# Five of eight activation transposes moved from TensorE to 32x32 block transposes on VectorE

## The chip, the core and the metric

The kernel runs on one core of a Trainium2 chip. The metric is the time of one execution on the device in microseconds; lower is better. A core has TensorE (PE, with its weight loads shown apart as PEld), VectorE (DVE), ScalarE (ACT), GpSimd (POOL) and SyncE (SP), which run their own programs in order and wait for each other through semaphores. SP and POOL issue the DMAs here, ACT four at the start.

## What is computed

Four batches of 512 tokens with 512 columns go through one layer of two halves, all in fp32:

```python
x = x + layernorm(attn(layernorm(x)))      # gated scan over the tokens
x = x + layernorm(ffn(layernorm(x)))

# attn: h [b, t, 512]
i, f, g = h @ Wi.T, h @ Wf.T, h @ Wg.T
gate = sigmoid(f);  v = silu(i) * (1 - gate)
o_t = gate_t * o_(t-1) + v_t               # associative scan over t
o = rmsnorm(o) * gnorm_w * g * sigmoid(g)
attn = einsum("btd,hd->bth", o, Wo)

# ffn: h [b, t, 512], 2048 hidden
hidden = silu(h @ W1.T) * (h @ W3.T)
ffn = hadamard(hidden) @ W2.T              # Walsh-Hadamard over the 2048
```

The kernel folds the Hadamard transform into W2. The products with Wi, Wf, Wg, W1 and W3 sum over the 512 columns of the normalized activations, so those must lie on the partitions: the normalized tile, with its tokens on the partitions, has to be transposed. There are two normalized tensors for each batch, called "a" (before attention) and "f" (before the FFN): eight transposes in all.

## The kernel before

**Products.** Every large product is done in seven block products instead of eight (Strassen-Winograd on a 2x2 split). `combine_left` and `combine_right` make the sums of blocks on DVE; `seven` returns the seven steps. A step is eight matmuls of 128x256, and its PSUM bank is then copied out by ACT (`nc.scalar.copy`, L348) or added in by DVE (L346). [...]

**Units.** `attn_unit(b, u)` is one of three attention units of batch b, `ffn_unit(b, m)` one of eight FFN units. Both call `project`, which runs the seven steps; after steps 1, 3, 5 and 6 (or after each, where `dense` is set, as in batch 0's FFN) `slot()` takes one piece of other work from the queue `fill`: the attention output of the next batch, the FFN output of this one, or the preparation of W2. The main loop runs over the batches b, and in it over m. After the eight FFN units of batch b come the three attention units of batch b+2, so that PE has work while DVE and ACT finish a batch. The attention units of batches 0 and 1 come ahead of the loop.

**Order.** The programs of PE and SP are in the order of the code (`manual_schedule`). Those of DVE, ACT and POOL are set by a scheduler from priorities and its own costs. `tc.high_priority` raises pieces of work.

**Normalizing.** `normalize_tiles` takes mean and variance on DVE (L244, L245), a power on POOL (L221) and writes (x - m) / s with one ACT instruction for each 128 tokens (L248) into a tile with tag "wide", of which there are three: xn, the attention output y and the FFN output f share them.

**Transposing.** `transpose` (L301) does 16 PE transposes of 128x128 into four PSUM banks (L309), two copies by ACT (L314), two by DVE (L316), and four combinations by DVE, at high priority. `xt`, the result, has two buffers. In the loop it is called for (b+2, "a") and (b+1, "f") one after the other at the end of each batch's FFN units, and for ("f", 3) alone at the end of batch 2.

**Weights.** `weight` loads a pair of column blocks of a weight from DRAM the first time (L157), 512 bytes for each row, with partition p holding rows p, 128 + p, 256 + p and 384 + p. DVE combines it, POOL stores it with its sums (`kept`, L138), and later batches load that (`again`, L145). In batch 0's FFN units SP's loads of new weights wait for buffers, and so for POOL's stores.

The functions that the change touches, and what calls them:

Of the kernel before, what the change touches and what calls it, by code (L numbers as in the profile page):

```python
# [11 lines left out]
F32 = mybir.dt.float32  # L12
AF = mybir.ActivationFunctionType
ALU = mybir.AluOpType
P = 128
# [12 lines left out]
B11, B21, B22, B12, T1, T2, T4 = range(7)  # L28
# [14 lines left out]
def kernel(  # L43
# [14 lines left out]
    nc = tc.nc  # L58
    B, T, D = x.shape
    FF = w1.shape[1]  # L60
    NT = T // P
    ND = D // P
    NF = FF // P
    NU = NF // 2
    NS = 2
    H = T // 2
# [7 lines left out]
    work = ctx.enter_context(tc.tile_pool(name="work", bufs=1))  # L74
    small = ctx.enter_context(tc.tile_pool(name="small", bufs=2))
    psum = ctx.enter_context(tc.tile_pool(name="psum", bufs=8, space=bass.MemoryType.PSUM))
    scratch = ctx.enter_context(
        tc.tile_pool(name="scratch", bufs=1, space=bass.MemoryType.DRAM)
    )
# [5 lines left out]
    def bank(name):  # L85
        return psum.tile([P, 2, H], F32, tag="ps", name=name)
# [18 lines left out]
    def flush():  # L105
        while fill:
            slot()


    xs = {}  # L110
# [16 lines left out]
    def combine_right(t, eng):  # L127

        eng.tensor_sub(t[:, T1], t[:, B12], t[:, B11])
        eng.tensor_sub(t[:, T2], t[:, B22], t[:, T1])  # L130
        eng.tensor_sub(t[:, T3], t[:, B22], t[:, B12])
        eng.tensor_sub(t[:, T4], t[:, B21], t[:, T2])
# [7 lines left out]
    def stream_tile(key, b, pool=stream):  # L140
        return pool.tile([P, 7, H], F32, tag="w", name="_".join(map(str, (*key, b))))

    def again(key, b, pool=stream):
        t = stream_tile(key, b, pool)
        nc.sync.dma_start(out=t, in_=saved[key])  # L145
        return t

    def weight(src, name, m, b):

        key = name, m  # L150
        if key in saved:
            return again(key, b).rearrange("p s (c f) -> p s c f", c=2)
        t = stream_tile(key, b)
        half = src.shape[1] // 2
        for h in range(2):
            cols = slice(h * half + m * P, h * half + (m + 1) * P)
            nc.sync.dma_start(  # L157
                out=t[:, 2 * h : 2 * h + 2].rearrange("p k (c f) -> p (k c) f", c=2),
                in_=src[:, cols].rearrange("(c p) f -> p c f", p=P),
            )  # L160
        uncombined.append((key, t))
        return t.rearrange("p s (c f) -> p s c f", c=2)
# [17 lines left out]
    def load_ffn_w(b, m):  # L180
        ffn_w[b, m] = weight(w1, "w1", m, b), weight(w3, "w3", m, b)
# [42 lines left out]
    def scales(mv, eps, name):  # L224

        n = mv.shape[1]
        r = inverse_root(mv, eps, name)
        nb = small.tile([P, n], F32, tag="nb", name=f"nb_{name}", bufs=4)
        i = nc.vector.scalar_tensor_tensor(nb, mv[:, :, 0], -1.0, r, ALU.mult, ALU.mult)
        return r, nb, i  # L230

    xns = {}

    def normalize_tiles(b, name, i0, n):

        if (name, b) not in xns:
            xns[name, b] = work.tile(
                [P, NT, D], F32, tag="wide", name=f"xn_{name}_{b}", bufs=3
            )
        t = xns[name, b]  # L240
        st = small.tile([P, n, 6], F32, tag=f"st{n}", name=f"st_{name}_{b}_{i0}")
        mv = small.tile([P, n, 2], F32, tag=f"mv{n}", name=f"mv_{name}_{b}_{i0}")
        for k in range(n):
            nc.vector.bn_stats(st[:, k, :], xs[b][:, i0 + k, :])  # L244
            nc.vector.bn_aggr(mv[:, k, :], st[:, k, :])  # L245
        r, nb, read["nb"] = scales(mv, EPS, f"{name}_{b}_{i0}")
        for k in range(n):
            nc.scalar.activation(  # L248
                t[:, i0 + k, :], xs[b][:, i0 + k, :], AF.Identity,
                bias=nb[:, k : k + 1], scale=r[:, k : k + 1],  # L250
            )

    def normalize(b, name, n=2):
        for i in range(0, NT, n):
            normalize_tiles(b, name, i, n)
# [43 lines left out]
    xts = {}  # L299

    def transpose(b, name):  # L301

        xn = xns.pop((name, b))
        xt = work.tile([P, 7, 2, H], F32, tag="xt", name=f"xt_{name}_{b}", bufs=2)
        pt = [bank(f"pt_{name}_{b}_{c}") for c in range(ND)]
        for h in range(2):
            for i in range(2 * h, 2 * h + 2):
                for c in range(ND):
                    nc.tensor.transpose(pt[c][:, h, ts(i % 2, P)], xn[:, i, ts(c, P)], ident)  # L309
        with tc.high_priority(offset=URGENT):  # L310
            for c in range(ND):
                to = xt[:, B11 : B12 + 1 : B12 - B11] if c < 2 else xt[:, B21 : B22 + 1]
                if c % 2:
                    nc.scalar.copy(to[:, :, c % 2, :], pt[c])  # L314
                else:
                    nc.vector.tensor_copy(to[:, :, c % 2, :], pt[c])  # L316
            combine_right(xt, nc.vector)
        xts[name, b] = xt


# [64 lines left out]
    def attn_unit(b, u, dense=False):  # L385
        def gates(d):

            v, gate = d[:, 0], d[:, 1]
            nc.scalar.activation(gate, gate, AF.Tanh, scale=0.5)
            nc.scalar.activation(v, v, AF.Silu)  # L390
            nc.vector.scalar_tensor_tensor(v, gate, 1.0, v, ALU.subtract, ALU.mult)
            nc.scalar.activation(gate, gate, AF.Identity, bias=half_t, scale=0.5)
            if u == 0:
                os_[b] = work.tile([P, 2, 2, T], F32, tag="o", name=f"o_{b}")
            for h in range(2):
                nc.vector.tensor_tensor_scan(
                    os_[b][:, u, h, :], gate[:, h, :], v[:, h, :], 0.0, ALU.mult, ALU.add
                )

        def output_gate(d):  # L400
            o = os_[b]
            og = work.tile([P, 7, 2, H], F32, tag="og", name=f"og_{b}")
            nc.scalar.activation(d, d, AF.Silu)
            for m in range(2):
                into_left(og, o[:, m], d[:, m], m)
            combine_left(og, nc.vector)
            ogs[b] = og
            nc.scalar.activation(o, o, AF.Square)
            nc.vector.tensor_add(o[:, 0], o[:, 0], o[:, 1])
            nc.vector.tensor_add(o[:, 0, 0], o[:, 0, 0], o[:, 0, 1])  # L410

        project(
            attn_w.pop((b, u)), xts["a", b], f"a_{b}_{u}", gates if u < 2 else output_gate,
            dense,
        )
# [52 lines left out]
    def ffn_unit(b, m, dense=False):  # L468
        def hidden(d):
            nc.scalar.activation(d[:, 0], d[:, 0], AF.Silu)  # L470
            ht = work.tile([P, 7, H], F32, tag="ht", name=f"ht_{b}_{m}", bufs=4)
            into_left(ht, d[:, 0], d[:, 1])
            combine_left(ht, nc.vector)
            hts[b, m] = ht

        project(ffn_w.pop((b, m)), xts["f", b], f"f_{b}_{m}", hidden, dense)
# [181 lines left out]
    for b in range(B):  # L658
        last = b == B - 1
        for m in range(NU):  # L660
            if m + 1 < NU:
                load_ffn_w(b, m + 1)
            if b == 0 and m % NS == 0:
                for k in range(m, m + NS):
                    fill.extend(transform_low(k))
            if m == 0 and not last:
                fill.extend([None] * 4 * (b > 0) + attn_out(b + 1))
            if m and m % NS == 0:
                if last and m == NU - NS:
                    fill.extend([None] * 8)  # L670
                fill.extend([None] + ffn_out(b, m // NS - 1))
            if m % NS == 1:
                load_down_w(b, m // NS)
            if m == 3 and b == 0:
                load_x(2)
            if m == 4 and b + 2 < B:
                normalize(b + 2, "a")
            ffn_unit(b, m, b == 0)
            combine_weights()
        tail = ffn_out(b, NU // NS - 1)  # L680
        if b + 2 < B:
            load_attn_w(b + 2, 0)
            transpose(b + 2, "a")
            transpose(b + 1, "f")
            fill.extend([None] + tail)
            for u in range(3):
                if u < 2:
                    load_attn_w(b + 2, u + 1)
                else:
                    load_ffn_w(b + 1, 0)  # L690
                attn_unit(b + 2, u)
            if b + 3 < B:
                load_x(b + 3)
        elif not last:
            load_ffn_w(b + 1, 0)
            transpose(b + 1, "f")
            fill.extend([None] + tail)
        else:
            fill.extend(tail)
            flush()  # L700
# [34 lines left out]
```

## Time and profile before

| | us |
|---|---|
| Median of 3 runs | 850.07 (849.54 to 850.56) |
| The profiled execution | 850.16 |
| Its span, first to last instruction | 848.2 |
| PE busy in the span | 824.5 (97%) |
| DVE / ACT / POOL busy | 452.7 (53%) / 263.5 (31%) / 60.6 (7%) |
| DMA moved | 159.06 MB, 187 GB/s from and to DRAM |
| Granted PE clock | 0.996 |

The profile is of one execution. A group of instructions is shown by line, engine, operation and tiles, with its count, busy time and mean; "idle before" is the time that its engine stood idle just ahead of it, with the instruction that ended the wait. A matmul's duration contains its latency, and matmuls overlap, so the time that a series takes is read from the starts of its neighbours or from the chain of work that ended last.

### The profile page before, as it was taken

Reading aid. Unit: us, or ns where it says so; the run is one execution under the profiler, and the core shown is the slowest. Engines: PE = TensorE matmul, PEld = TensorE weight load, DVE = VectorE, ACT = ScalarE, POOL = GpSimd, SP = SyncE. Lnnn points to the kernel's source line nnn. Section 1 sums busy time; section 2 is a strip of 40 time slices with the busy share of each in tenths; the row PEclk is TensorE's granted clock in tenths of the full one; section 3 lists DMA queues with packets and bytes.
Section 4 is the critical chain, followed back from the end, with each engine's and each line's share of the span. In section 5 each row is a group of like instructions: output and inputs, shape, how many; then the busy total and the mean of one; then the engine's idle time right before and its main releaser. Section 6 shows DMA issues by size and latency. Waiting matters only on the chain.

```text
span 848.2 us, 9895 instructions
## 1 busy us (share of the span) xinstructions
PE 824.5 (97%) x3808; PEld 710.1 (84%) x3808; DVE 452.7 (53%) x904; ACT 263.5 (31%) x386; POOL 60.6 (7%) x102
## 2 busy tenths in 40 slices
PE   6999999999999999999999999999999999999995
PEld 3778878888878888888888888888888888888884
DVE  5557686765564646537333645737334533633445
ACT  4454462433221224326211222524221211222111
POOL 4110110111100001002000000101000000100000
PEclk9999999999999999999999999999999999999998
DMA  9985376677778224826324322844251633625101
GB/s 339 402 308 216 134 271 230 223 273 273 273 287 326 87 87 171 361 88 236 128 114 188 116 87 87 301 182 174 87 208 43 270 140 122 223 88 216 49 40 50
DMA packets 53744, 159.06 MB, mean 188 GB/s; under 512 B 4289, under 2 KB 29505, under 8 KB 53697
## 3 DMA queue, kind: packets, MB, share of 16 engines
q1 hardware_dynamic: 45968, 120.40, 38.9%
q0 software_dynamic: 7008, 36.71, 10.8%
q10 hardware_dynamic: 720, 1.31, 0.4%
q8 instruction: 30, 0.49, 0.2%
q14 instruction: 18, 0.14, 0.0%
HBM read 120.66 MB, written 37.75 MB: 187 GB/s over the span
## 4 chain that ended last, share of the span: by engine, by line
PE 69%; DVE 2%; DMA 1%; ACT 1%; issue 1%; SPq 0%; POOLq 0%; DVEq 0%
PE X_f L361 21%; PE X_po L494 11%; PE Z_f L361 11%; PE Z_po L494 6%; PE Y_f L361 5%; PE X_a L361 5%; PE Y_po L494 3%; PE Z_a L361 2%; PE X_y L447 2%; PE Y_a L361 1%; PE Z_y L447 1%; DMA w<-in_W_dram 1%; DMA s_w<-w 1%; DVE f L346 0%; PE Y_y L447 0%
## 5 line engine op out<-in xcount | busy, mean ns | idle before, releaser
L361 PE MATMUL X_f<-xt_f,w 128*128 128x256 f32 x1024 | 241.9, 380 | 1.7 <-DVE xt_f L316 1.2
L361 PEld LDWEIGHTS X_f<-xt_f,w 128*128 128x128 f32 x1024 | 194.0, 190 | 32.5 <-issue 3.8
L348 ACT COPY d_f<-X_f 128x512 f32<-128x512 f32 x96 | 56.0, 584 | 306.1 <-PE X_f L361 281.7
L494 PE MATMUL X_po<-w,ht 128*128 128x256 f32 x512 | 120.9, 379 | 0.2 <-DVE f L346 0.2
L361 PE MATMUL Z_f<-xt_f,w 128*128 128x256 f32 x512 | 120.9, 379 | 0.0
L361 PEld LDWEIGHTS Z_f<-xt_f,w 128*128 128x128 f32 x512 | 97.3, 190 | 14.9 <-issue 1.0
L494 PEld LDWEIGHTS X_po<-w,ht 128*128 128x128 f32 x512 | 97.2, 190 | 13.7 <-DVE f L346 0.6
L346 DVE TENSOR_TENSOR f<-X_po,f 128x512 f32<-128x512 f32 x51 | 35.2, 689 | 97.0 <-PE X_po L494 96.9
L376 DVE TENSOR_TENSOR ht<-d_f 128x1024 f32<-128x1024 f32 x32 | 39.0, 1220 | 74.6 <-ACT d_f L470 55.4
L494 PE MATMUL Z_po<-w,ht 128*128 128x256 f32 x256 | 60.6, 379 | 1.5 <-DVE f L346 1.5
L361 PE MATMUL Y_f<-xt_f,w 128*128 128x256 f32 x256 | 60.5, 379 | 0.0
L494 PEld LDWEIGHTS Z_po<-w,ht 128*128 128x128 f32 x256 | 48.6, 190 | 8.5 <-DVE f L346 1.9
L361 PEld LDWEIGHTS Y_f<-xt_f,w 128*128 128x128 f32 x256 | 48.6, 190 | 8.3 <-issue 1.2
L348 ACT COPY d_a<-X_a 128x512 f32<-128x512 f32 x36 | 21.0, 584 | 92.4 <-PE X_a L361 76.3
L221 POOL TENSOR_TENSOR rs_f<-rs_f,power 128x2 f32<-128x2 f32 x16 | 14.6, 915 | 476.8 <-DVE nm_f L282 443.0
L346 DVE TENSOR_TENSOR d_f<-Z_f,d_f 128x512 f32<-128x512 f32 x32 | 22.1, 690 | 27.2 <-PE Z_f L361 27.2
L346 DVE TENSOR_TENSOR d_f<-X_f,d_f 128x512 f32<-128x512 f32 x32 | 22.1, 690 | 27.0 <-PE X_f L361 27.0
L361 PE MATMUL X_a<-xt_a,wi 128*128 128x256 f32 x128 | 33.1, 381 | 1.7 <-DVE xt_a L316 1.7
L470 ACT ACTIVATE d_f<-d_f 128x1024 f32<-128x1024 f32 x32 | 33.8, 1055 | 0.9
L361 PE MATMUL X_a<-xt_a,wf 128*128 128x256 f32 x128 | 32.9, 379 | 0.0
L346 DVE TENSOR_TENSOR f<-Z_po,f 128x512 f32<-128x512 f32 x28 | 19.3, 689 | 24.6 <-PE Z_po L494 24.6
L361 PE MATMUL X_a<-xt_a,wg 128*128 128x256 f32 x128 | 30.4, 381 | 1.4 <-DVE d_a L346 0.8
(150 smaller groups left out, 997.0 us busy)
## 6 DMA issues: line engine op xcount, KB each, us to landing
w<-s_w SPq DMA_DIRECT2D x80, 896.0 KB, 6.2
s_w<-w POOLq DMA_DIRECT2D x24, 896.0 KB, 4.8
w<-in_W_dram SPq DMA_DIRECT2D x32, 256.0 KB, 5.8
wi<-s_wi SPq DMA_DIRECT2D x6, 896.0 KB, 9.7
wf<-s_wf SPq DMA_DIRECT2D x6, 896.0 KB, 6.7
wg<-s_wg SPq DMA_DIRECT2D x6, 896.0 KB, 5.9
wo<-s_wo SPq DMA_DIRECT2D x6, 896.0 KB, 8.2
w_h<-w2p POOLq DMA_DIRECT2D x8, 512.0 KB, 7.3
```

Source lines behind the costliest of these rows:

```text
L221: read["power"] = nc.gpsimd.tensor_tensor(r, r, power_t[:, 0:n], ALU.pow)
L346: read[what] = nc.vector.tensor_add(to, ps[which], to)
L348: nc.scalar.copy(to, ps[which])
L361: nc.tensor.matmul(ps[:, n, :], w[:, a, c, :], xt[:, bb, c, :], start=first and n == 0 and c == 0, stop=c == 1, skip_group_check=True,)
L376: nc.vector.tensor_mul(to.rearrange("p (t k) f -> p k t f", t=2), a.rearrange("p k (t f) -> p k t f", t=2), b2.rearrange("p k (t f) -> p k ...
L447: nc.tensor.matmul(ps[:, t, :], og[:, a, c, ts(t, P)], w[c][:, bb, :], start=first and t == 0 and c == 0, stop=c == 1, skip_group_check=True,)
L470: nc.scalar.activation(d[:, 0], d[:, 0], AF.Silu)
L494: nc.tensor.matmul(ps[:, t, :], hts[b, m][:, a, ts(t, P)], w[m][:, bb, :], start=first and t == 0 and m == ms[0], stop=m == ms[-1], skip_g ...
```

## The change

Three of the eight transposes stay on PE: "a" of batches 0 and 1 and "f" of batch 0 (`ON_TENSOR`), all ahead of the main loop. The other five go another way:

1. ACT writes the normalized columns in another order, and POOL stores the tile to DRAM (`xnd`), in two DMAs of 512 KB.
2. `load_fold` loads it back on SP in four DMAs of 256 KB, one for each group of 32 partitions, in pieces of 512 bytes. Partition 32 i + q then holds columns 128 i to 128 i + 127 (in the new order) of every token whose number is q modulo 32. The tile has the tag "wide".
3. `transpose_fold` transposes 32x32 blocks on DVE, four instructions of 512 columns, which gives xt; the four combinations follow. Neither has a raised priority.

For block transposes to give rows that match, the 512 columns are dealt to the partitions as p = column // 4, so the weights' rows are loaded so too, and the three tensors that stay on PE are written by ACT with the matching order. In the loop, the fold that is needed first after batch b ("a" of b+2, or "f" of 3) is loaded at m = 6 and transposed at m = 7; "f" of b+1 is loaded after the units, ahead of the second attention unit's weights, and transposed ahead of that unit.

```diff
@@ weight @@
-                in_=src[:, cols].rearrange("(c p) f -> p c f", p=P),
+                in_=src[:, cols].rearrange("(p c) f -> p c f", p=P),
@@ normalize_tiles @@
+    ON_TENSOR = ("a", 0), ("a", 1), ("f", 0)
...
         for k in range(n):
+            x_t, to = xs[b][:, i0 + k, :], t[:, i0 + k, :]
+            if (name, b) in ON_TENSOR:
+                x_t = x_t.rearrange("p (k c) -> p c k", c=ND)
+                to = to.rearrange("p (c k) -> p c k", c=ND)
+            else:
+                x_t = x_t.rearrange("p (i a c) -> p i c a", c=ND, a=32)
+                to = to.rearrange("p (i c a) -> p i c a", c=ND, a=32)
             nc.scalar.activation(
-                t[:, i0 + k, :], xs[b][:, i0 + k, :], AF.Identity,
-                bias=nb[:, k : k + 1], scale=r[:, k : k + 1],
+                to, x_t, AF.Identity, bias=nb[:, k : k + 1], scale=r[:, k : k + 1]
+            )
+        if (name, b) not in ON_TENSOR:
+            if (name, b) not in xnd:
+                xnd[name, b] = scratch.tile(
+                    [NT, P, D], F32, tag=f"xn_{name}_{b}", name=f"xnd_{name}_{b}"
+                )
+            nc.gpsimd.dma_start(
+                out=xnd[name, b][i0 : i0 + n].rearrange("t p d -> p t d"),
+                in_=t[:, i0 : i0 + n, :],
             )
@@ new @@
+    def load_fold(b, name):
+        folds[name, b] = t = work.tile(
+            [P, T // 32, P], F32, tag="wide", name=f"fold_{name}_{b}", bufs=3
+        )
+        rows = xnd[name, b].rearrange("t p d -> (t p) d")
+        for i in range(4):
+            nc.sync.dma_start(
+                out=t[ts(i, 32)],
+                in_=rows[:, ts(i, P)].rearrange("(g q) k -> q g k", q=32),
+            )
+
+    def transpose_fold(b, name):
+        fold = folds.pop((name, b)).rearrange("p (h g) k -> p h g k", h=2)
+        xt = work.tile([P, 7, 2, H], F32, tag="xt", name=f"xt_{name}_{b}", bufs=2)
+        for c in range(ND):
+            to = xt[:, B11 : B12 + 1 : B12 - B11] if c < 2 else xt[:, B21 : B22 + 1]
+            nc.vector.transpose(
+                to[:, :, c % 2, :].rearrange("p h (g q) -> p h g q", q=32),
+                fold[:, :, :, ts(c, 32)],
+            )
+        combine_right(xt, nc.vector)
+        xts[name, b] = xt
@@ main loop @@
+            if m == 6 and not last:
+                load_fold(*((b + 2, "a") if b + 2 < B else (b + 1, "f")))
+            if m == NU - 1 and not last:
+                transpose_fold(*((b + 2, "a") if b + 2 < B else (b + 1, "f")))
             ffn_unit(b, m, b == 0)
...
         if b + 2 < B:
             load_attn_w(b + 2, 0)
-            transpose(b + 2, "a")
-            transpose(b + 1, "f")
+            load_fold(b + 1, "f")
             fill.extend([None] + tail)
             for u in range(3):
...
+                if u == 1:
+                    transpose_fold(b + 1, "f")
                 attn_unit(b + 2, u)
...
         elif not last:
             load_ffn_w(b + 1, 0)
-            transpose(b + 1, "f")
             fill.extend([None] + tail)
```

More of the change, by code (lines that the diff above doesn't have):

```diff
@@ L230, in scales @@
         return r, nb, i
-    xns = {}
+    xns, xnd = {}, {}
+    ON_TENSOR = ("a", 0), ("a", 1), ("f", 0)
     def normalize_tiles(b, name, i0, n):
@@ L317, in transpose @@
             combine_right(xt, nc.vector)
+        xts[name, b] = xt
+    folds = {}
+    def load_fold(b, name):
[18 more added lines that the diff above has]
+        combine_right(xt, nc.vector)
         xts[name, b] = xt
```

## The prediction

> **What bounds the kernel now.** I read the page first: busy times, then the chain that ended last.
>
> ```profile
> span 848.2 us, 9895 instructions
> ...
> PE 824.5 (97%) x3808; PEld 710.1 (84%) x3808; DVE 452.7 (53%) x904; ACT 263.5 (31%) x386; POOL 60.6 (7%) x102
> ...
> PE 69%; DVE 2%; DMA 1%; ACT 1%; issue 1%; SPq 0%; POOLq 0%; DVEq 0%
> ```
>
> TensorE is busy for 97% of the span, and of the chain no other engine holds more than 2%. DVE, ACT and POOL have room. So a PE instruction taken out shortens the run by its own pitch, provided nothing else becomes late in its place. The groups view, shapes kept apart, has the rows that go and the row that changes (busy, mean ns | idle before):
>
> ```profile
> L248 ACT ACTIVATE xn_f<-x,nb_f,rs_f 128x512 f32<-128x512 f32 x16 | 12.5, 808 | 14.8 <-DVE nb_f L229 14.8
> ...
> L309 PE MATMUL pt_f<-ident,xn_f 128*128 128x128 f32 x64 | 7.9, 273 | 0.1
> ...
> L316 DVE COPY xt_f<-pt_f 128x512 f32<-128x512 f32 x8 | 5.3, 686 | 1.8 <-PE pt_f L309 1.8
> ...
> L314 ACT COPY xt_f<-pt_f 128x512 f32<-128x512 f32 x8 | 4.3, 587 | 3.2 <-PE pt_f L309 3.2
> ```
>
> The 273 ns is a latency; matmuls overlap. The price in time is the pitch, which the chain in order of time gives:
>
> ```profile
> 282.23 1.75 PE pt_a L309 x16
> 283.98 1.75 PE pt_f L309 x16
> 285.73 1.73 PE X_a L361 x8
> ```
>
> Sixteen transposes cost 1.75 us, and after the first batch's two sets the matmuls go on without a gap. Then the timeline, for what PE waits for around transposes and at the start (start, duration, idle before and its releaser):
>
> ```profile
> 11.38 2.93 ACT L248 ACTIVATE xn_a<-x,nb_a,rs_a 128x512 f32<-128x512 f32 x4
> ...
> 12.24 2.77 PE L309 MATMUL pt_a<-ident,xn_a 128*128 128x128 f32 x16 [1.39 <-ACT xn_a L248]
> ...
> 15.47 1.13 PE L361 MATMUL X_a<-xt_a,wi 128*128 128x256 f32 x4 [0.46 <-DVE xt_a L316]
> ...
> 107.87 1.99 PE L361 MATMUL X_a<-xt_a,wg 128*128 128x256 f32 x8 [0.62 <-ACT d_a L348]
> ...
> 233.64 1.99 PE L494 MATMUL Z_po<-w,ht 128*128 128x256 f32 x8 [1.51 <-DVE f L346]
> ...
> 475.30 1.40 PEld L309 LDWEIGHTS pt_f<-ident,xn_f 128*128 128x128 f32 x13 [0.37 <-ACT xt_a L314]
> ...
> 674.25 1.99 PE L361 MATMUL X_f<-xt_f,w 128*128 128x256 f32 x8 [0.75 <-DVE xt_f L316]
> ```
>
> The last two are PE idle caused by the transposes that go: 0.37 for banks that ACT has not yet emptied, 0.75 for xt's copies. The first three lines are a part of the kernel where PE runs behind ACT: the four L248 activations, 0.73 us apart, set when the first matmuls can start.
>
> [...] No DVE transpose is in this trace. [...] The new activations read fp32 at a step of four elements[...]; no row of this trace reads so. [...] The trace's nearest loads, w<-in_W_dram with the same 512-byte pieces and 256 KB, land in 5.8 us (median).
>
> **The change, part by part.**
>
> *Transposes taken off PE.* Five sets (a of batches 2 and 3, f of 1, 2 and 3), 5 x 16 transposes: 5 x 1.75 = -8.75. The program of the changed kernel has 80 PE rows fewer and the same matmuls in the same order. The waits of 0.37 and 0.75 go with them: -1.12. What is late next at these places is nothing that I can see: each fold's transposes are issued in unit 7 or in the attention unit before the first use, a unit of 11 products x 1.73 = 19 us ahead.
>
> *DVE.* Per set it loses two copies of 686 ns and gains four block transposes[...] What hides it is idle DVE: over 434 to 454 us, where the set of batch 3 goes, DVE is busy 7.5 of 20 us. The transposes carry normal priority and stand in DVE's program between evacuations, which come 3 to 5 us apart there. Cost 0; if that cover fails, up to 0.5 us a set. ACT loses ten copies of 587 ns, off the path.
>
> *Stores (POOL).* Two per set, 512 KB, ten at the 0.53 to 0.58 us that POOL takes for s_w; POOL is 7% busy. Behind the first store of an f stands the pow of its second half, and DVE waits for that. In batch 2 the store can go at 392.2 plus whatever ACT adds, the pow ran at 394.1: no wait. In batch 0 the two a-stores (about 213 to 216 us) go ahead of w2's block 5, whose landing at 222.5 SP waits for before it loads unit 6's weights; that is the chain behind the 1.51 us at 233.64. One 896 KB store (w1's block 5) moves behind it in exchange, so 1.0 MB instead of 0.9 stands in front: +0.3, between -1.5 (the gap closes) and +3.
>
> *Loads (SP).* Four per set, 20 in all, at 0.6 us (four w<-in_W_dram took 2.45): 12 us on a queue that mostly waits for PE. Behind the a-folds stand w2's blocks 6 and 7, behind the f-folds the next attention unit's weights, needed a unit later. DMA carries 10.5 MB more on 159. Cost 0.
>
> *Weights in another row order.* Same bytes and pieces; the rows of one partition are now adjacent. Zero, plus or minus 1 us: the first wi and wf are combined at 14.3, a us before use.
>
> *Strided reads on ACT, all 32 of L248.* Let each cost d more. The floor is 0; [...] nothing shows a gain. Most lie beside other work, about ten do not. At the start four in a row precede the first matmul: 4d. At 44 us one delays a bank's copy (gap 0.74): 1d. At 103 to 108 two precede the copy behind the 0.62 of line 107.87: 2d. At 111 two delay the gate, the scan and the evacuation behind a gap of 0.81 at 115.9: 2d. In batch 0's FFN, where every product has a filler behind it, I count one more. 10d: [...] I take the middle, d = 0.2: +2.0.
>
> Sum: -8.75 - 1.12 + 0 + 0.3 + 2.0 = -7.6. The profiled execution took 850.16 (span 848.2 and 2.0 around it), so 842.6; the median shown, 850.07, is 0.1 lower: **842.5**.
>
> **Rivals.** *Half-rate reads on ACT.* [...] Against: the four activations at the start might partly hide behind weights not yet combined. *Free reads.* d = 0: 840.5. [...]
>
> *Folds land late: slower.* DVE works in order; while the first block transpose waits for its four loads, the evacuations behind it wait, and PE runs on for about two products (3.5 us) before it lacks a bank. In batch 1 the fold's loads can go when unit 5's weights are freed, about 437 us, and the transposes stand behind the evacuation of 450.7 to 451.4: slack 14 us. To end slower by 0.2%, five places must cost 7.6 + 1.7 = 9.3, so 1.9 each, so DVE held for 5.4: a landing of 20 us. Median landings of all such weight loads lie between 5.8 and 13.5 us, the latter at the crowded start, and DMA's share is 0.13 in that stretch. At 22 us each, PE would stand 22 - 14 - 3.5 = 4.5 us at five places: 842.5 + 22.5 = 865. Little speaks for it.
>
> That the change does nothing is excluded by the program; that PE's time is handed to another wait, the row order included, would end near 850.
>
> **How the numbers follow.** What tells from no change is about 0.2%, 1.7 us. Chances: forecast (d of 0.1 to 0.3) 0.42; half rate 0.27; free 0.17; near no change 0.06; late folds or another slower end 0.08. The first three are faster: 0.86. Range: from the free reads with the gap at 233 closed (839.2) to half rate with 2 us of new waits (846.8), which leaves out the last 0.14 and a little at each end.
>
> **What would show it.** PE near 816 us busy with L309 at 48 pairs; no PE wait behind xt from 250 us on. L248's mean gives d: 808 free[...]; the first X_a starts at 15.5 + 4d. [...] the wait list shows DVE xt <- DMA fold only if the last rival is right. I am wrong if PE has new gaps at 255 to 300, 445 to 490 or 650 to 680 us, or if the gap near 233 has grown past 3 us.

## The result, and the profile after

| | us |
|---|---|
| Changed kernel, median of 12 runs | 849.99 (847.98 to 852.63) |
| Kernel before, beside it | 850.19 (849.14 to 851.36) |
| Ratio | 0.9999 (0.9987 to 1.001) |
| The profiled execution of the changed kernel | 848.68, span 846.9, clock 0.996 |

Forecast was 842.5, faster. What came is no change. Single executions of the changed kernel also differ in the TensorE clock they were granted: five at a mean of 0.995 or 0.996 have their middle at 848.7 us, seven at 0.993 or less at 850.6, so the profile (0.996) lies 1.3 us below the median.

First the page of the changed kernel: busy times and the chain of work that ended last.

```profile
span 846.9 us, 9792 instructions
...
PE 817.6 (97%) x3728; PEld 701.1 (83%) x3728; DVE 459.0 (54%) x914; ACT 274.3 (32%) x376; POOL 69.4 (8%) x112
...
PE 81%; DVE 6%; DMA 4%; ACT 4%; issue 2%; POOL 1%; SPq 0%; POOLq 0%; ACTq 0%; DVEq 0%
```

TensorE has its 80 instructions fewer and is 6.9 us less busy, yet the span is only 1.3 us shorter: PE's waiting grew. The two chains can't be compared share by share. This one covers the whole span, and ACT and DVE hold 10% of it; the one printed before the change begins at 211 us, so its shares come to about 75% of the span, and what held PE up before 211 us is not in them. ACT lost ten copies and is still 10.8 us busier. The groups, shapes kept apart (busy, mean ns | idle before), say why:

```profile
L262 ACT ACTIVATE xn_f<-x,nb_f,rs_f 128x512 f32<-128x512 f32 x16 | 20.8, 1325 | 15.1 <-DVE nb_f L229 12.3 <-DMA w<-s_w 2.8
L262 ACT ACTIVATE xn_a<-x,nb_a,rs_a 128x512 f32<-128x512 f32 x16 | 20.4, 1320 | 5.2 <-DVE nb_a L229 5.2
L367 DVE STREAM_TRANSPOSE xt_f<-fold_f 128x512 f32<-128x512 f32 x12 | 7.7, 682 | 0.0
L367 DVE STREAM_TRANSPOSE xt_a<-fold_a 128x512 f32<-128x512 f32 x8 | 5.4, 692 | 0.0
```

The activation (L248 before, L262 now) went from 805 and 808 to 1320 and 1325 ns. The DVE transposes take 682 and 692 ns, and DVE never stood idle for them (0.0 in the last column).

Where this reaches TensorE is in the timeline (start, duration, idle before and its releaser):

```profile
11.96 4.92 ACT L262 ACTIVATE xn_a<-x,nb_a,rs_a 128x512 f32<-128x512 f32 x4
...
18.05 1.13 PE L415 MATMUL X_a<-xt_a,wi 128*128 128x256 f32 x4 [0.45 <-DVE xt_a L341]
...
111.55 1.99 PE L415 MATMUL X_a<-xt_a,wg 128*128 128x256 f32 x8 [1.63 <-ACT d_a L402]
...
124.78 0.70 PE L415 MATMUL X_f<-xt_f,w 128*128 128x256 f32 x2 [0.46 <-DVE xt_f L341]
...
176.61 1.99 PE L415 MATMUL X_f<-xt_f,w 128*128 128x256 f32 x8 [0.18 <-ACT d_f L402]
...
240.51 1.99 PE L548 MATMUL Z_po<-w,ht 128*128 128x256 f32 x8 [1.78 <-DVE f L400]
...
409.81 1.99 PE L415 MATMUL X_f<-xt_f,w 128*128 128x256 f32 x8 [0.67 <-ACT d_f L402]
...
672.26 1.89 PE L415 MATMUL X_f<-xt_f,w 128*128 128x256 f32 x8
...
835.00 1.89 PE L548 MATMUL X_po<-w,ht 128*128 128x256 f32 x8
```

Two of the same products before the change:

```profile
120.05 0.70 PE L361 MATMUL X_f<-xt_f,w 128*128 128x256 f32 x2 [0.46 <-DVE xt_f L316]
...
837.10 1.89 PE L494 MATMUL X_po<-w,ht 128*128 128x256 f32 x8
```

Read each start against the same product before. The first product (18.05) starts 2.58 us later, the one at 111.55 (before 107.87) 3.68 later, the first X_f of the main loop (124.78 against 120.05) 4.73 later, the one at 240.51 (233.64) 6.87 later. From there the trend turns: PE's last group of matmuls ends 2.10 earlier (835.00 + 1.89 against 837.10 + 1.89). So 6.9 us are lost in the first 240 us, and 9.0 gained in the rest. The waits of 0.37 and 0.75 around the transposes at 475 and 674 are gone, as the line at 672.26 (no bracket) shows for the second.

### The profile page after: what moved, and what is told of

Same layout as the page of the kernel before. It is cut to its first block, busy times and chain, and to the rows that moved or that the text cites. A ratio compares the mean times of both kernels' runs of the same rounds, so it can differ in the third digit from the quotient of the medians.

```text
span 846.9 us, 9792 instructions
## 1 busy us (share of the span) xinstructions
PE 817.6 (97%) x3728; PEld 701.1 (83%) x3728; DVE 459.0 (54%) x914; ACT 274.3 (32%) x376; POOL 69.4 (8%) x112
## 4 chain that ended last, share of the span: by engine, by line
PE 81%; DVE 6%; DMA 4%; ACT 4%; issue 2%; POOL 1%; SPq 0%; POOLq 0%; ACTq 0%; DVEq 0%
PE X_f L415 23%; PE X_po L548 11%; PE Z_f L415 11%; PE X_a L415 8%; PE Z_po L548 6%; PE Y_f L415 5%; PE Z_a L415 4%; PE X_y L501 3%; PE Y_po L548 3%; PE Y_a L415 2%; PE Z_y L501 2%; ACT xn_a L262 1%; DMA wi<-s_wi 1%; DMA x<-in_x_dram 1%; PE Y_y L501 1%
## 5 line engine op out<-in xcount | busy, mean ns | idle before, releaser
L415 PEld LDWEIGHTS X_a<-xt_a,wi 128*128 128x128 f32 x128 | 24.1, 190 | 8.1 <-issue 3.3
```

The costliest lines, as they stand in the source:

```text
L415: nc.tensor.matmul(ps[:, n, :], w[:, a, c, :], xt[:, bb, c, :], start=first and n == 0 and c == 0, stop=c == 1, skip_group_check=True,)
```

## The experiments

**Theory:** ACT's reads at a step of four elements cost far more than the 0.2 us assumed, and where PE runs behind ACT this gives the saving back. **Rival:** the detour gives it back (stores, fold loads, queue positions, DVE transposes, the weights' row order). The times below are medians; the ratio is to the kernel before, run beside them. In e_three_strided, e_two_strided, e_steps and e_rows_alone the columns do not match the weights' rows, so what they compute is not the layer; the instructions and their sizes are the same.

| Kernel | us | Ratio, 95% |
|---|---|---|
| e_runs32 | 841.12 | 0.9900 (0.9885 to 0.9914) |
| e_m5 | 842.03 | 0.9906 (0.9891 to 0.9920) |
| e_two_strided | 842.91 | 0.9913 (0.9900 to 0.9927) |
| e_three_plain | 844.40 | 0.9932 (0.9920 to 0.9944) |
| e_a1_fold | 845.61 | 0.9942 (0.9929 to 0.9954) |
| e_write | 845.92 | 0.9948 (0.9935 to 0.9962) |
| e_three_strided | 847.27 | 0.9965 (0.9950 to 0.9979) |
| e_rows_alone | 850.14 | 1.0003 (0.9995 to 1.0011) |
| e_steps | 850.33 | one execution |
| e_late_load | 850.52 | 1.0008 (0.9996 to 1.0021) |
| e_rows_only | 851.10 | 1.0014 (1.0007 to 1.0021) |
| e_stride_only | 856.57 | 1.0074 (1.0062 to 1.0086) |

**The detour without the reads at a step (e_runs32).** Block transposes only need the 512 columns dealt out in groups of 32. With p = column mod 128, partition group i of the fold can hold runs of 32 neighbouring columns, and the weights keep their old rows.

```diff
-                in_=src[:, cols].rearrange("(p c) f -> p c f", p=P),
+                in_=src[:, cols].rearrange("(c p) f -> p c f", p=P),
...
-            if (name, b) in ON_TENSOR:
-                x_t = x_t.rearrange("p (k c) -> p c k", c=ND)
-                to = to.rearrange("p (c k) -> p c k", c=ND)
-            else:
-                x_t = x_t.rearrange("p (i a c) -> p i c a", c=ND, a=32)
+            if (name, b) not in ON_TENSOR:
+                x_t = x_t.rearrange("p (c i a) -> p i c a", c=ND, a=32)
                 to = to.rearrange("p (i c a) -> p i c a", c=ND, a=32)
```

> The detour through DRAM and the DVE block transposes stay for the five sets, but ACT reads runs of 32 columns (128 bytes) for them and whole rows for the other three, and the weights' rows are back in their old order. Theory (ACT's reads at a step of four elements give the time back): the normalizing activations return to about 0.81 us, the first projection starts near 15.5 us again, the 9.9 us of transposes and waits saved stay saved: 840 to 841.5. Rival (the detour itself costs: stores, loads, queue positions, DVE transposes): it stays above 846, near 850.

841.12 us. Its groups:

```profile
L259 ACT ACTIVATE xn_f<-x,nb_f,rs_f 128x512 f32<-128x512 f32 x16 | 12.6, 809 | 15.1 <-DVE nb_f L229 15.1
L259 ACT ACTIVATE xn_a<-x,nb_a,rs_a 128x512 f32<-128x512 f32 x16 | 12.2, 806 | 4.8 <-DVE nb_a L229 4.8
```

Theory held. With the reads in runs of 32 the activation is back at its old time, and 9.06 us of the 9.87 stay. Every part of the detour is still there, so by this sum it costs about 0.8. This is the fastest of the kernels here. Its profile is of its slowest execution (844.45): ACT's first activation began at 12.54 there, so the first product came at 16.64 and not near 15.5, the gap near 233 us was 2.43, and PE's next products came slowly behind it (2.75 us instead of 1.73, last section).

**The reads without the detour (e_stride_only).** The kernel before, all eight sets on PE, in the new column order (with the weights' rows to match).

```diff
             nc.scalar.activation(
-                t[:, i0 + k, :], xs[b][:, i0 + k, :], AF.Identity,
+                t[:, i0 + k, :].rearrange("p (c k) -> p c k", c=ND),
+                xs[b][:, i0 + k, :].rearrange("p (k c) -> p c k", c=ND), AF.Identity,
```

> The kernel before with nothing but the column order: ACT writes all eight tensors at the new order (reads at a step of four), weights' rows to match, all eight transposes on TensorE, no store and no fold. Theory (strided reads): slower than before by what the changed kernel gave back, 7 to 8 us: 857 to 858; the activations take 1.32 us each, the first projection starts near 18.05. Rival (detour costs): within 1.5 us of before, 850 to 851.5.

856.57, so 6.4 slower than before, a little under the forecast and far from the rival. Its activations take 1323 and 1325 ns. In its profile the first X_f starts at 126.40, 6.35 later than before. Not all of that is ACT: the granted clock was 0.77 from 10 to 20 us and 0.89 from 20 to 30, which is an estimated loss of up to 3.4 us (0.23 and 0.11 of 10 us each). A part of the loss is absorbed later, since the gap of 1.5 us at 233 is gone in its trace (what it waited for has time to arrive).

**Which tensors: the three ahead of the loop (e_three_plain, e_three_strided).** The first takes the step away from them alone: ACT writes whole rows, and PE's transposes read every fourth column (`xn[:, i, c::ND]`). The second adds the step to them alone, in e_runs32.

> The changed kernel, but the three tensors that stay on TensorE are written by ACT as whole rows, and TensorE picks every fourth column as it transposes; the five folded sets keep the strided reads and the weights keep the new row order. Theory: the losses ahead of the main loop (4.7 us by the shift of the last product before it) go, those of batch 0's FFN and later (2.1 and 0.7) stay: 850.0 - 4.7 = 845.3, first projection near 15.5 us. Rival (weights' row order or the detour causes them): stays at 849 to 851.

> The version with runs of 32 columns, but the three tensors ahead of the main loop are read by ACT at a step of four (their columns so do not match the weights); the five folded ones keep the runs of 32. Theory (the parts add up: the changed kernel less the version with whole rows for these three gave 5.6, its trace shows 4.1 to 4.7): 841.1 + 4.1 to 5.6 = 845.2 to 846.7, with the four activations of the start taking 4.92 us instead of 2.93. Rival (the losses do not add, the fast loop absorbs a part): below 844.5.

844.40 is 5.6 below the changed kernel, 0.9 more than expected; the first product starts at 15.50. The other way round it costs 6.2 (847.27), above the 4.1 to 5.6 expected, in executions from 844.54 to 851.15. Both misses go with the granted clock. Over the executions where it was 0.995 or more, the middle is 848.7 for the changed kernel, 844.4 for e_three_plain, 845.6 for e_three_strided and 841.1 for e_runs32, so the three tensors cost 4.3 taken away and 4.5 put in, of 7.6 that the reads cost together. The greater part of the loss comes from three tensors that the change does not even move off TensorE.

**Which tensors: the eight activations beside batch 0's FFN (e_two_strided).**

```diff
+            if (name, b) in (("f", 1), ("a", 2)):
+                x_t = x_t.rearrange("p (i a c) -> p i c a", c=ND, a=32)
+                to = to.rearrange("p (i c a) -> p i c a", c=ND, a=32)
```

> The version with runs of 32 columns, but f of batch 1 and a of batch 2 are read at a step of four; their eight activations run beside batch 0's FFN (those two tensors' columns so do not match the weights). Theory (four of these eight activations are felt, by the 2.1 us that the changed kernel's products lost between 125 and 240 us): 841.1 + 2.1 = 843.2. Rival one (the prediction's count, one of the eight): 841.6. Rival two (those 2.1 us have another cause, such as the weights' row order): 841.1.

842.91: 1.8 more than e_runs32, between the forecast of 2.1 and the rival's 0.5, and nearer the first. The prediction's count of one falls. The timelines of ACT show how f's activations are felt; first e_runs32, then this kernel:

```profile
169.64 0.81 ACT L259 ACTIVATE xn_f<-x,nb_f,rs_f 128x512 f32<-128x512 f32 x1 [0.57 <-DVE nb_f L229]
170.36 0.56 ACT L399 COPY d_f<-X_f 128x512 f32<-128x512 f32 x1
170.82 0.81 ACT L259 ACTIVATE xn_f<-x,nb_f,rs_f 128x512 f32<-128x512 f32 x1
...
172.06 0.58 ACT L399 COPY d_f<-Z_f 128x512 f32<-128x512 f32 x1
```

```profile
170.32 1.33 ACT L262 ACTIVATE xn_f<-x,nb_f,rs_f 128x512 f32<-128x512 f32 x1 [1.11 <-DVE nb_f L229]
171.56 0.57 ACT L402 COPY d_f<-X_f 128x512 f32<-128x512 f32 x1
172.02 1.33 ACT L262 ACTIVATE xn_f<-x,nb_f,rs_f 128x512 f32<-128x512 f32 x1
...
173.72 0.59 ACT L402 COPY d_f<-Z_f 128x512 f32<-128x512 f32 x1
```

Two activations stand closely ahead of copies that free banks (the kernel's pool has eight), in ACT's own order, and PE's next products wait 0.19 each for those copies. Each such stop moves PE's later starts by 0.45, more than the wait itself: the wait is counted from the end of a matmul's duration, which contains its latency, and a product that starts after a stop is 0.1 us longer (1.99 instead of 1.89). Against the kernel before, PE's starts slip by 1.40 us in three steps between 171 and 177, and by 0.48 more at 213, where a of batch 2 is normalized: 1.88 together.

**What about a read at a step costs (e_steps, e_write).** In the first, batch b reads at a step of 1, 2, 4 or 8; in the second the changed kernel's loops are turned round, so that ACT reads in order and writes at a step:

```diff
-                x_t = x_t.rearrange("p (k c) -> p c k", c=ND)
-                to = to.rearrange("p (c k) -> p c k", c=ND)
+                x_t = x_t.rearrange("p (k c) -> p k c", c=ND)
+                to = to.rearrange("p (c k) -> p k c", c=ND)
             else:
-                x_t = x_t.rearrange("p (i a c) -> p i c a", c=ND, a=32)
-                to = to.rearrange("p (i c a) -> p i c a", c=ND, a=32)
+                x_t = x_t.rearrange("p (i a c) -> p i a c", c=ND, a=32)
+                to = to.rearrange("p (i c a) -> p i a c", c=ND, a=32)
```

> The kernel before, with ACT's reads in normalizing at a step of 1, 2, 4 and 8 elements for batches 0, 1, 2 and 3, and contiguous writes (columns so come out in an order that does not match the weights). Theory[...]: 0.81 us at step 1, part of the 0.515 at step 2, 1.32 at 4, and no more than 1.32 at 8. Rival (any step other than one costs the same): 1.32 at 2, 4 and 8. Rival (it grows with the distance): 8 costs clearly more than 4.

> The changed kernel with the same column order, weights' rows and folds, but ACT's loops turned round: it reads x in its natural order and writes at a step (every 128th column for the three tensors on TensorE, every 32nd for the five folded ones). Theory ([...] writes at a step are free): the activations take 0.81 us, 841 to 842.5. Rival (any access at a step costs ACT the same, on whichever side): the activations take 1.3 us, 849 to 851.

ACT's timeline of e_steps, at a step of 1, 2, 2, 4 and 8:

```profile
12.23 2.93 ACT L249 ACTIVATE xn_a<-x,nb_a,rs_a 128x512 f32<-128x512 f32 x4
44.45 0.84 ACT L249 ACTIVATE xn_a<-x,nb_a,rs_a 128x512 f32<-128x512 f32 x1 [3.96 <-DVE nb_a L229]
...
46.88 1.63 ACT L249 ACTIVATE xn_a<-x,nb_a,rs_a 128x512 f32<-128x512 f32 x2
...
388.17 1.34 ACT L249 ACTIVATE xn_f<-x,nb_f,rs_f 128x512 f32<-128x512 f32 x1 [2.78 <-DVE nb_f L229]
...
398.07 4.92 ACT L249 ACTIVATE xn_a<-x,nb_a,rs_a 128x512 f32<-128x512 f32 x4
```

Step 2 costs 0.03 to 0.05 us (single durations 0.84 to 0.86), step 4 costs 0.5, and step 8 no more than step 4 (4.92 for four, as at step 4). So the price does not grow with distance from 4 to 8, and not every step has it. These are the times that the theory named, with little of the 0.515 at step 2; what sets the price was not shown, and a step of 3 was not tried. Of e_write:

```profile
11.91 4.41 ACT L262 ACTIVATE xn_a<-x,nb_a,rs_a 128x512 f32<-128x512 f32 x4
45.60 1.26 ACT L262 ACTIVATE xn_a<-x,nb_a,rs_a 128x512 f32<-128x512 f32 x1 [3.96 <-DVE nb_a L229]
```

Neither forecast of its time came: 845.92 lies in the middle. Writes at a step are not free (means 1.27 and 1.29 instead of 0.81, near the rival's 1.3), but four in a row take 4.41 against 4.92 for reads.

**The row order (e_rows_only, e_rows_alone).** The kernel before with the new row order and PE's transposes reading every fourth column; then with the new row order alone.

> The kernel before with the weights' rows in the new order and TensorE picking every fourth column in its transposes; ACT writes whole rows, nothing else is changed. Theory: no change, 850 within 1 us. Rival (adjacent rows in one partition make the first loads slower, or TensorE reads every fourth column more slowly): 852 or more, with the first projection later than 16 us or a transposes' pitch over 1.75 us for 16.

> The kernel before with nothing but the weights' rows loaded in the new order (transposes as before, so the columns do not match the weights). Theory (the 0.9 us that rows and TensorE's reads at a step cost together are TensorE's: 1.93 us instead of 1.75 for sixteen transposes, five sets in the loop): 850.2, the same as before. Rival (the row order costs it): 851.1, as with both.

851.10 and 850.14. The row order alone costs nothing that these executions can tell (ratio 1.0003, 0.9995 to 1.0011). Both together are slower by 0.9, between theory and rival. That is PE's: in the chain of e_rows_only sixteen transposes that load every fourth column take longer than the 1.75 of before, and in its trace PE's starts slip by 0.36 and 0.33 at the two places in the loop where two sets follow each other; the single set near 674 shows no slip. The rest of the 0.9 is not shown.

```profile
285.00 1.92 PE pt_a L309 x16
286.92 1.94 PE pt_f L309 x16
```

**How far the fold is covered (e_a1_fold, e_late_load, e_m5).** Three variants of e_runs32: a of batch 1 folded too; the loop's folds loaded at m = 7 instead of 6; a of batch 2 normalized at m = 5.

> The version with runs of 32 columns, and a of batch 1, ahead of the main loop, goes by the fold too: its loads stand on SP ahead of wi and wf of batch 1, its DVE transposes in the place of TensorE's. Theory (an exposed DVE wait is the limit there): the 1.75 us of transposes go, and the gap of 1.3 us ahead of batch 1's first product shrinks to 0.5 or less if the loads land 3 us before: 838.5 to 839.5. Rival (DMA is nearly full in the first 100 us, so the fold lands late and TensorE waits): 841 to 845, with a DVE wait on the fold near 65 us.

> The version with runs of 32 columns, but the folds of the main loop are loaded at m = 7, in SP's queue behind w2's blocks 6 and 7, instead of m = 6 ahead of them; their DVE transposes stay where they were. In that version the last of such loads lands some 4 us before the DVE transposes in batch 0 and 10 us in batch 1. Theory (the detour is free only as long as that cover lasts, and DVE works in order): the loads land after the transposes' turn, DVE waits on them, and TensorE behind it: 843 to 848, a DVE wait on the fold in the waits. Rival (what stands behind the transposes on DVE is not urgent): within 0.7 of 841.1.

> The version with runs of 32 columns, with a of batch 2 normalized and stored at m = 5 of batch 0's FFN instead of m = 4, so that its two 512 KB stores stand behind w2's block 5 on POOL instead of ahead of it. Theory (the stores lengthen the gap near 233 us, 2.4 us in that version's profile, 1.5 before): the gap shrinks below 1.5, and 840 to 840.5. Rival (the gap is set by other transfers): 841 to 841.5, with a gap of 1.5 or more.

In e_a1_fold the rival held, and 845.61 is 0.6 past its range. This is the prediction's slower rival (late folds) at work, in a place where DMA is nearly full (share 1.0 and more in the last section's windows):

```profile
65.01 2.49 DVE L364 STREAM_TRANSPOSE xt_a<-fold_a 128x512 f32<-128x512 f32 x4 [2.86 <-DMA fold_a<-xnd_a]
...
67.00 2.04 PE L412 MATMUL X_a<-xt_a,wi 128*128 128x256 f32 x4 [3.85 <-DVE xt_a L364]
```

Behind this wait, up to 73.5 us, PE's starts slip by another 3.4 us against e_runs32, at the low clock of the last section (0.67 and 0.64).

e_late_load lost all the gain, but not as the theory had it: DVE nowhere waits for a fold. With the load later the scheduler put the four transposes late in DVE's program, behind ht's work, and PE stands 2.90 us at 470 (below) and again at 668. In e_runs32 the same transposes began at 451.57, more than 20 us ahead of the product. PE's starts slip by 3.28 and 3.27 there, 6.6 of the 9.4 us lost. The rest goes with the granted clock: executions at 0.997 took 848.0 to 848.2, which leaves about 0.5, the others up to 855.0.

```profile
470.34 1.23 DVE L427 TENSOR_TENSOR ht<-d_f 128x1024 f32<-128x1024 f32 x1 [2.74 <-ACT d_f L521]
...
472.41 2.49 DVE L364 STREAM_TRANSPOSE xt_a<-fold_a 128x512 f32<-128x512 f32 x4
...
473.22 1.25 PE L412 MATMUL X_a<-xt_a,wi 128*128 128x256 f32 x4 [2.90 <-issue]
```

e_m5 lies above both of its forecasts (842.03; its ratio's interval overlaps that of e_runs32), and its gap near 233 is 1.92 us: nothing shows that the order of those stores sets it.

## Why the prediction was wrong, step by step

*Transposes and waits, -9.87: right.* From 240.51 to PE's last matmul the changed kernel gains 8.97, in spite of new slips of 0.94 at 409 and 0.19 at 591, so 10.10 (3.50 at 285, 3.84 at 476, 2.76 at 674); e_runs32 keeps 9.06 of it at the end.

*DVE, loads, row order at 0: right.* A transpose took 682 to 692 ns, like one of the copies that went (684 and 686 before), and DVE is busy 6.3 us more in all (459.0 against 452.7). No DVE wait on a fold is among the changed kernel's waits. The cover was thinner than written, though: in e_runs32's trace the f-fold of batch 1 is issued by 274.05 us, folds of f land within 13.4, and its transposes start at 288.88: by these figures as little as 1.4 us of cover.

*Stores, +0.3: not contradicted, but not shown.* The gap at 233 went from 1.51 to 1.78. That the size fits is luck: in profiles with the stores in the same place it is 1.36 (e_late_load) to 2.43 (e_runs32), in e_rows_alone and e_rows_only, without them, 0.89 and 1.06.

*Strided reads, 10d = +2.0: the step that failed, mostly by d.* d measured 0.515 (1320 less 805), more than twice the 0.2 of the sum. No row of the trace before showed such a read, so the 0.2 was the author's estimate, the middle between free and a "half rate" that was not shown; the 846.8 at the end of the range rests on that half rate too. Ten at 0.315 more are 3.15. The count of ten was short too. Ahead of the loop PE's starts slip by 1.99 at the start (4.92 less 2.93), 0.44 at 44, -0.45 at 66 (a wait for xt that shrank), 1.11 and 1.05 at 103 to 116, so 4.14 for the nine counted. But they slip by 1.88 beside batch 0's FFN, where one was counted, by 0.94 in batch 1 and by 0.19 in batch 2, where none was: there too activations stood ahead of a bank's copy in ACT's order. Together 7.15, about fourteen times d: 2.0 more.

*Not in the sum:* in the changed kernel's profile ACT began at 11.96, not 11.38, and PE's starts are 0.6 later from there. This start lies anywhere from 11.02 (e_stride_only) to 13.66 (e_rows_only) in the profiles, so it is chance and not the change. The time from PE's last matmul to the end of the span is 10.0 us instead of 9.2. That 0.8 is in every one of the profiles with folds and in none without; what fills it the records do not show.

The sum with these: 842.6 + 3.15 + 2.0 + 0.6 + 0.8 - 0.23 (10.10 for 9.87) = 848.9; the profile has 848.68. These terms were read from that profile, so the sum shows that nothing large is left out, and no more; that the reads are the cause rests on e_runs32 and e_stride_only. The median lies 1.3 us above the profile, with a lower clock.

*A reading that was too wide, and a sum.* The prediction read the shares of the chain as if they were those of the whole span. That chain begins at 211 us, so the stretch where ACT sets PE's pace, and where 4.14 of the 7.15 were lost, has no part in "of the chain no other engine holds more than 2%"; the timeline was what showed those places. The low end of the range, 839.2, does not come out of its terms either: free reads with the gap closed give 838.7.

*The rivals.* Half-rate reads named the cause, ACT's reads at a step, with a price that no trace had shown and a count of ten where about fourteen were felt. "PE's time is handed to another wait" named the outcome at 850, but not which wait, and had a chance of 0.06. Late folds did not happen here; e_a1_fold shows that they can. Of the signs named, L262's mean and the late first product came; new gaps in the three listed stretches did not.

## What to carry to other kernels

A change that moves work off the busiest engine is paid for where the data are prepared: cost every instruction whose access pattern changes, also those on a path that the change seems to leave alone, and ask which of them stands ahead of a bank's copy in its engine's own order. An operand at a new step is a new operation (1.32 us here instead of 0.81); when no row shows it, measure it first or choose an order that keeps runs together (32 columns were enough here, at 0.81 us, and the weights' rows could stay). The place of the transposes in DVE's program mattered as much here as the landing of their data: PE stood 2.90 us behind four that came late in it (e_late_load), 3.85 behind four that waited for a fold (e_a1_fold).

## What the runs showed of the hardware

ACT, 512 fp32 columns from SBUF to SBUF: 0.81 us in order or in runs of 32 (e_runs32), 0.84 to 0.86 at a read step of 2 and 4.92 for four in a row at 8 (e_steps), 1.32 and, for four in a row, 4.92 at 4 (the changed kernel); writing at a step of 32 or 128 elements 1.27 to 1.29 (e_write). PE's 128x128 fp32 transposes go from 1.75 us for sixteen (the kernel before) to 1.92 and 1.94 when every fourth column is loaded (e_rows_only). A DVE transpose of 32x32 blocks takes 0.68 to 0.69 us for 128x512 fp32 (the changed kernel).

After a longer wait of TensorE the granted clock was low for some microseconds in several profiles. The windows of e_a1_fold after its wait of 3.85 us (PE busy, PEld, DVE, ACT, POOL, then PEclk, DMA share, GB/s), and those of e_three_strided at its start:

```profile
65.00:70.00 5.00, 2.99 (x6) 2.01 (x7) 4.99 (x7) 0.94 (x2) 0.00 (x0) 0.67 1.02 406
70.00:75.00 5.00, 5.00 (x16) 4.07 (x15) 5.00 (x8) 2.16 (x2) 0.00 (x0) 0.64 1.05 428
75.00:80.00 5.00, 4.59 (x22) 3.73 (x22) 5.00 (x14) 1.76 (x3) 0.53 (x1) 1.00 0.56 237
```

```profile
10.00:20.00 10.00, 7.26 (x23) 4.31 (x22) 5.51 (x14) 7.06 (x8) 5.86 (x11) 0.69 1.06 382
```

In 70 to 75 us PE is busy throughout and does 16 matmuls where e_runs32 does 25 in the same window at a clock of 1.00. The starts show where it was slow. Four matmuls of 128x256 are followed by the next four after 0.86 us otherwise (74.82 to 75.68 in e_a1_fold), but after 1.87 and 1.71 in e_a1_fold (starts at 69.05, 70.92 and 72.63) and in e_stride_only (17.25, 19.12 and 20.83). Eight are followed by the next after 1.73 us otherwise, but after 2.75 in e_runs32 behind its wait of 2.43 (235.72 to 238.47), and after 3.39 in e_m5 behind its wait of 1.92 (234.39 to 237.78).

It doesn't come each time: the changed kernel's profile has a wait at its start like that of e_three_strided (1.88 against 1.90) and a clock of 1.00 there, and e_late_load's profile has two waits of 2.90 with products at their usual distance soon behind them (four matmuls 0.87 after 474.30, eight 1.73 after 673.26). Over all executions, mean clocks were 0.989 to 0.998 with the step in the first four reads (e_three_strided, e_stride_only, the changed kernel), and 0.995 to 0.997 in e_three_plain, e_two_strided and e_runs32 without it. But e_late_load (0.989 to 0.997) and e_a1_fold (0.993 to 0.995) go low without it and have longer waits elsewhere, and e_rows_only had 0.83 at 10 to 20 us with ACT's reads as before. That waits of TensorE cause it fits most of these, but was not isolated.
